# Two-layer graph attention and relation sums: the norm between the layers folded into weights, evictions moved to ScalarE, list writes spread

## The chip, the cores and the metric

The kernel runs on one core of a Trainium2 chip. The metric is the device time of one launch in microseconds; before the change it is 2796.56 us, the median of three runs (2795.64 to 2802.76). The profile is of one further execution. Engines are called PE (matrix multiplies; PEld is its weight load), DVE (the vector engine), ACT (the scalar engine), POOL (GpSimd) and SP (which only issues transfers).

## The reference

There are 1250 nodes with 768 features, 20000 edges sorted by their destination, and 34 edge types. What is computed, cut to what matters:

```python
def gatv2(x, src, dst, Ws, bs, Wd, bd, attn):          # H heads of D features
    fs = (x @ Ws + bs).reshape(-1, H, D)
    fd = (x @ Wd + bd).reshape(-1, H, D)
    logits = einsum('ehd,hd->eh', leaky_relu(fs[src] + fd[dst], 0.2), attn)
    alpha = softmax of logits over the edges of a destination
    return elu(segment_sum(alpha[:, :, None] * fs[src], dst, N))

h   = relu(layernorm(x))
h1  = gatv2(h, ..., W1s, b1s, W1d, b1d, attn1)          # 8 heads of 96
h1  = layernorm(h1 + h) * ln1_w + ln1_b
out = gatv2(h1, ..., Wos, bos, Wod, bod, attno)         # 1 head of 768
x   = x + layernorm(out) * lno_w + lno_b
h   = relu(layernorm(x))
# relation layer: mean over the edges of a type, W_rel[type], sum over types, + h @ W_root + b_rgcn;
# then @ W_gcn, a degree-weighted sum over neighbours, + b_gcn, + x
```

A node without edges has a sum of zero in gatv2, so its elu is zero. Since the attention weights of a node add to one, a constant row added to every fs adds that row to the sum of every node that has edges.

## The kernel before

Nodes are sorted by their number of in-edges and cut into ten tiles of 128. Tile k has as many *slots* as its largest node has edges: 33, 22, 20, 18, 17, 16, 15, 14, 13, 11, in all 179. One slot holds one edge of each of the tile's 128 nodes. Tiles with more than 20 slots are cut into two *chunks* (16 and 17, 11 and 11), so there are twelve chunks.

**Front of the program** (0 to about 150 us): edges are ranked, h and the source rows fs = h @ W1s + b1s are written to memory (f_h0_d and f_fs_d; bias by a matmul of a row of ones with the bias row, line 814).

**First attention** (about 150 to 910 us; `attention(H, ...)`, line 1172, with 8 heads). For a slot, `front` gathers 128 source rows from memory by POOL's indirect transfer (line 1148) into one of 24 ring buffers, and DVE computes max(fs, -fd) (line 1208), the product with attn (1213) and a sum by head (1214). After a chunk's fronts, `softmax` gives the weights, ACT doing the exponent (1232). `back` multiplies the rows by their weights (ACT, eight instructions of 96 columns, line 1266; for the last tile mostly DVE) and PE adds them up in PSUM with two matmuls by the identity (1268). The backs of one chunk alternate with the fronts of the next. `end` then divides by the softmax sum (`share`, line 1276), adds the two chunks of a tile, applies elu and calls `finish1`.

`negated1` (line 1409 on) makes a tile's -fd: POOL gathers h, PE transposes it and multiplies it by W1d, and DVE evicts it from PSUM with the sign and the bias (line 1416). It is called by `begin(j + 2)`, in the middle of chunk j. `finish1` (line 1420 on) adds h, normalizes (statistics on DVE, scaling on ACT, line 1425), multiplies by ln1_w and adds ln1_b (DVE, 1426 and 1427), transposes, multiplies by Wos, evicts with the bias bos (DVE, 1433), makes the row sums of fs times attno, which stand in column 768 (DVE, 1435), scatters fs2 to memory (POOL), multiplies by Wod and evicts with the sign and bod (DVE, 1440). Both denses and negated1's use the one PSUM buffer "mm2". Wos and Wod and five rows, each spread over all 128 partitions, are loaded by `loads1`, called at slot 3 of the first chunk.

**Second attention** (about 910 to 1384 us): the same function with one head. DVE has two instructions a slot (1208, and 1210, which also accumulates), ACT makes a diagonal matrix of the weights (1256) and PE sums with two matmuls (1258). `finish2` (line 1459 on) normalizes, adds x, normalizes again, scatters h2, and multiplies by W_root; it has two elementwise operations (1467, 1470), a gather and two scatters on POOL for each tile.

**List writes.** POOL also writes 179 scatters of 12-byte records into r_pair_d (line 1152), the lists by type which the relation stage reads at its start, after both attentions. `list_edges(row, slots)` adds `slots` to a due counter and issues a write right behind the gather `row` for each whole one. `attention` has two arguments for it: `rate` is added for each slot (not for the first 20 of tile 0), and `rest` once at the last slot. The first attention has 0.9 and 60, the second 0 and 0: 143 writes lie between the gathers of the first attention and 36 behind its last gather.

**Relation stage** (1394 to about 2575 us) and the last sums (to the end) follow; PE sets the pace in the former.

The order of the instructions on an engine is made when the program is built, from the order in which they are written and from where a planner expects an engine to stand idle; so a finish's matmuls have some of the next backs among them. Each engine then runs its own list in order.

Of the kernel before, what the change touches and what calls it, by code (L numbers as in the profile page):

```python
# [10 lines left out]
F32 = mybir.dt.float32  # L11
# [615 lines left out]
def fast_front(ctx, tc, f, x, src, dst, edge_type, W1s, b1s, W1d, b1d, attn1, attno, W_rel):  # L627
# [52 lines left out]
    with ExitStack() as front:  # L680
# [33 lines left out]
        ones_row = early.tile([1, P], F32, name="ones_row")  # L714
# [10 lines left out]
        f.bias_1 = const.tile([P, D], F32, name="bias_1")  # L725
        nc.scalar.dma_start(f.bias_1, bass.AP(tensor=b1d.tensor, offset=b1d.offset, ap=[[0, P], [1, D]]))
# [399 lines left out]
def fast_rest(ctx, tc, f, x, src, dst, edge_type, W1s, b1s, W1d, b1d, attn1, ln1_w, ln1_b,  # L1126
# [45 lines left out]
    def attention(H, table, negated, attn_e, first, loads, finish, rate, rest):  # L1172
# [98 lines left out]
        def share(o, ps, by):  # L1271

            if H == 1:
# [8 lines left out]
        def end(t):  # L1282
# [4 lines left out]
            share(o, c.ps, c.den)  # L1287
# [35 lines left out]
        for j, now in enumerate(chunks):  # L1323
            after = chunks[j + 1] if j + 1 < len(chunks) else None
            for i in range(max(now.n, after.n if after else 0)):
                if i < now.n and after:
                    back(now, i)
                if after and i < after.n:
                    front(after, i)
                if i == now.n // 2:  # L1330
                    begin(j + 2)
            if after:
# [4 lines left out]
            if now.first + now.n == now.t.S:  # L1337
# [7 lines left out]
                            f.degf[:, :, None].to_broadcast([P, NT, S0]), op=ALU.is_ge)  # L1345

# [50 lines left out]
    with ExitStack() as one:  # L1397
        bias_1 = f.bias_1
        late = {}

        def loads1():
            ap1 = late["pool"] = one.enter_context(tc.tile_pool(name="r_att1", bufs=1, side="right"))
            late["wos"], late["wod"] = load_w(ap1, Wos, "wos", "wos"), load_w(ap1, Wod, "wod", "wod")
            for name, a in (("lnw", ln1_w), ("lnb", ln1_b), ("bias_s", bos), ("bias_d", bod), ("attn_o", attno)):
                late[name] = load_row(ap1, a, name)
# [3 lines left out]
        def negated1(k, nfd):  # L1409
# [5 lines left out]
            ps = dense(nc, ps_t, f, hT, f.w1d, 0, P, tag="mm2")  # L1415
            nc.vector.scalar_tensor_tensor(
                nfd.rearrange("p (a h) d -> p a h d", a=2), ps[:, :, :HW].rearrange("p a (h d) -> p a h d", d=D // H),
                -1.0, bias_1.rearrange("p (a h d) -> p a h d", a=2, d=D // H), op0=ALU.mult, op1=ALU.subtract)

        def finish1(k, o):  # L1420
            lnw, lnb, wos, wod = late["lnw"], late["lnb"], late["wos"], late["wod"]
            bias_s, bias_d, attn_o = late["bias_s"], late["bias_d"], late["attn_o"]
# [3 lines left out]
            nc.vector.tensor_mul(o, o, lnw)  # L1426
            nc.vector.tensor_add(o, o, lnb)
            hT = pool.tile([P, KC, P], F32, name="hT1", tag="hT1", bufs=1)
            to_columns(nc, ps_t, f, hT, 0, o, P)
            ps = dense(nc, ps_t, f, hT, wos, 0, P, tag="mm2")  # L1430
            ap1 = late["pool"]
# [296 lines left out]
```

## Time and profile before

| what | value |
|---|---|
| median of three runs | 2796.56 us |
| profiled execution, its own time | 2795.48 us |
| its span | 2793.7 us |
| mean granted clock of PE | 0.925 |
| busy share of PE, DVE, ACT, POOL | 84%, 56%, 30%, 55% |
| first gather of the first, of the second attention | 152.9, 908.8 us |
| last gather of the first, of the second attention | 813.4, 1307.5 us |
| first gather of the relation stage | 1394.6 us |

A row of the groups names line, engine and operation, out<-in with the shapes, the count, then the busy time and the mean in ns of one, then the idle time of the engine just before them and what ended most of it. "issue" is idle time for which the trace shows no wait, "remote" a wait whose releaser it doesn't show. Consecutive DVE instructions overlap by some 0.08 us in these records. Matmuls of fp32 are two records each.

### The profile page before, as it was taken

The numbers are of one execution on the slowest core, as the hardware profiler recorded it, in microseconds if no ns is written. First come the engines' busy times: TensorE is split into PE (matmuls) and PEld (weight loads), VectorE is DVE, ScalarE is ACT, GpSimd is POOL, SyncE is SP. The second block draws the span as 40 slices with busy tenths as digits, with TensorE's granted clock in tenths as the row PEclk, the third lists the DMA queues.
The fourth block names the chain that finished last, engine by engine and source line by source line (L and its number), as shares of the span: only waits on it lengthen the run. The fifth ranks groups of instructions, "written<-read, shape, count | busy, mean of one in ns | idle before, by whom it ended". The sixth has DMA issues, their size and how long they took to land. (4 is left out here: it accounts for less than half of the span.)

```text
span 2793.7 us, 23960 instructions
## 1 busy us (share of the span) xinstructions
PE 2345.4 (84%) x7635; PEld 1354.2 (48%) x7635; DVE 1556.5 (56%) x2363; ACT 851.2 (30%) x2295; POOL 1546.9 (55%) x1131
## 2 busy tenths in 40 slices
PE   5953693788988377898789999999999999999667
PEld 3521252444444244454456666666666666665234
DVE  6589969898985899999453222222222222200263
ACT  3003774776772122333311211221221122121000
POOL 1343877777774766776275444444444544431574
PEclk9976896999999789999889999999999999999888
DMA  6144443454531766765387777777777777765785
GB/s 214 45 159 164 131 129 94 120 142 129 143 102 35 267 208 193 220 208 182 123 264 191 190 191 190 186 195 198 197 188 185 194 192 182 182 158 147 235 275 182
DMA packets 137988, 483.91 MB, mean 173 GB/s; under 512 B 26474, under 2 KB 28803, under 8 KB 137854
## 3 DMA queue, kind: packets, MB, share of 16 engines
q0 software_dynamic: 85152, 341.52, 47.1%
q1 hardware_dynamic: 48043, 134.21, 13.6%
q10 hardware_dynamic: 4658, 6.57, 0.7%
q8 instruction: 63, 1.03, 0.1%
q14 instruction: 72, 0.58, 0.1%
HBM read 392.99 MB, written 89.33 MB: 173 GB/s over the span
## 5 line engine op out<-in xcount | busy, mean ns | idle before, releaser
L1116 PE MATMUL ps<-wrel,mT 128*128 128x384 f32 x3336 | 1099.6, 486 | 1.3 <-DMA wrel<-in_L_gnn_W_rel_dram 1.3
L1116 PEld LDWEIGHTS ps<-wrel,mT 128*128 128x128 f32 x3336 | 623.4, 190 | 407.5 <-issue 1.6
L1148 POOL DMA_INDIRECT g<-r_h_d,lists x241 | 340.8, 1414 | 527.6 <-DVE g L1580 282.8
L1268 PE MATMUL ag<-fs,identf 128*128 128x384 f32 x716 | 291.1, 541 | 178.0 <-ACT fs L1266 167.8
L1580 DVE TENSOR_TENSOR g<-g,g 128x768 f32<-128x768 f32 x68 | 64.6, 950 | 620.4 <-DMA g<-r_h_d,lists 304.0
L1208 DVE TENSOR_TENSOR z<-fs,nfd 128x776 f32<-128x776 f32 (+1 forms) x358 | 347.4, 988 | 45.3 <-DMA fs<-f_fs_d,rec 24.9
L1266 ACT ACTIVATE fs<-fs,lg 128x96 f32<-128x96 f32 x1376 | 371.1, 362 | 4.6 <-issue 4.1
L1258 PE MATMUL ag<-fs,dg 128*128 128x384 f32 x716 | 252.4, 514 | 80.6 <-ACT dg L1256 80.0
L1148 POOL DMA_INDIRECT fs<-f_fs_d,rec x179 | 245.0, 1369 | 104.6 <-issue 48.1
L1152 POOL DMA_INDIRECT r_pair_d<-rec,place x179 | 245.8, 1373 | 95.0 <-issue 47.9
L1268 PEld LDWEIGHTS ag<-fs,identf 128*128 128x128 f32 x716 | 136.4, 205 | 321.1 <-ACT fs L1266 244.4
L1603 POOL DMA_INDIRECT r_h_d<-y,lists x139 | 221.8, 1596 | 109.3 <-ACT y L1602 52.9
L1148 POOL DMA_INDIRECT fs<-r_fs_d,rec x179 | 234.9, 1312 | 83.2 <-issue 33.1
L1258 PEld LDWEIGHTS ag<-fs,dg 128*128 128x128 f32 x716 | 142.1, 201 | 187.6 <-ACT dg L1256 85.7
L1602 ACT ACTIVATE y<-ps,lists 128x768 f32<-128x768 f32 x71 | 64.1, 902 | 479.8 <-PE ps L1116 473.0
L1602 ACT ACTIVATE y<-ps,rcnt 128x768 f32<-128x768 f32 x68 | 61.4, 902 | 456.3 <-PE ps L1116 456.3
L1659 DVE TENSOR_TENSOR acc<-acc,nb 128x768 f32<-128x768 f32 x86 | 82.4, 958 | 198.1 <-DMA nb<-r_h_d,srcz 194.2
L1210 DVE SCALAR_TENSOR_TENSOR z<-z,attn_o 128x769 f32<-128x769 f32 x179 | 178.4, 1015 | 0.0
L1213 DVE TENSOR_TENSOR z<-z,attn 128x776 f32<-128x776 f32 x179 | 168.8, 958 | 0.1
L1214 DVE TENSOR_REDUCE lg<-z 128x8 f32<-128x776 f32 x179 | 168.4, 953 | 0.1
L1513 DVE SCALAR_TENSOR_TENSOR arow<-node,from_f,arow 128x1250 f16<-128x1250 f16 x93 | 140.3, 1508 | 1.0
L1104 PEld LDWEIGHTS pt<-identf,g 128*128 128x128 f32 x834 | 100.5, 142 | 55.2 <-issue 24.1
(284 smaller groups left out, 2301.8 us busy)
## 6 DMA issues: line engine op xcount, KB each, us to landing
wrel<-in_L_gnn_W_rel_dram SPq DMA_DIRECT2D x37, 2304.0 KB
g<-r_h_d,lists POOLq DMA_INDIRECT x241
r_nfd_d<-fd SPq DMA_DIRECT2D x10, 384.0 KB
nfd<-r_nfd_d SPq DMA_DIRECT2D x10, 384.0 KB
r_x_d<-xb SPq DMA_DIRECT2D x10, 384.0 KB
x1r<-r_x_d SPq DMA_DIRECT2D x10, 384.0 KB
f_fs_d<-o_s SPq DMA_DIRECT2D x9, 388.0 KB
x<-in_x_dram SPq DMA_DIRECT2D x9, 384.0 KB
```

The lines of the kernel that those rows point to most:

```text
L1116: last = nc.tensor.matmul(ps[:n, half, :f.HW], hT[:, k, j * P:j * P + n], w[:, k, cols], start=(k == 0), stop=(k == f.KC - 1 and not bias))
L1148: return nc.gpsimd.indirect_dma_start(out=to, out_offset=None, in_=table, in_offset=bass.IndirectOffsetOnAxis(ap=idx, axis=0))
L1152: s = nc.gpsimd.indirect_dma_start(out=table, out_offset=bass.IndirectOffsetOnAxis(ap=idx, axis=0), in_=rows, in_offset=None, **kw)
L1208: nc.vector.tensor_tensor(z, fs, t.nfd, op=ALU.max)
L1210: nc.vector.scalar_tensor_tensor(z[:, 0, :], z[:, 0, :], 1.0, attn_e[:, 0, :], op0=ALU.mult, op1=ALU.mult, accum_out=t.lg[:, s, :])
L1213: nc.vector.tensor_mul(z, z, attn_e)
L1214: nc.vector.tensor_reduce(t.lg[:, s, :], z, axis=AX.X, op=ALU.add)
L1258: nc.tensor.matmul(c.ps[:, half, :HW], dg, fs[:, 0, half * HW:(half + 1) * HW], start=begin, stop=end)
L1266: nc.scalar.activation(fs[:, h, :HD], fs[:, h, :HD], AF.Copy, scale=t.lg[:, s, h:h + 1])
L1268: nc.tensor.matmul(c.ps[:, half, :HW].rearrange("p (h d) -> p h d", d=HD), f.identf, fs[:, half * H // 2:(half + 1) * H // 2, :HD], start= ...
L1513: nc.vector.scalar_tensor_tensor(a, node16, from_f[:, k, s:s + 1], a, op0=ALU.is_equal, op1=ALU.add)
L1603: s = nc.gpsimd.indirect_dma_start(out=h1_d[:, :], out_offset=bass.IndirectOffsetOnAxis(ap=j.node, axis=0), in_=y, in_offset=None, compute ...
```

## The change

It has six parts.

1. `finish1` no longer multiplies by ln1_w and adds ln1_b. `fold(0)` and `fold(1)`, called at slots 5 and 9 of the first chunk's backs (so while the second chunk's fronts run), scale the rows of Wos and Wod by ln1_w in place (ACT, six instructions of 768 columns each). ln1_b @ Wos + bos and ln1_b @ Wod + (ln1_b @ Wos + bos) + bod are made by one-row matmuls and copied out by ACT. ln1_w and ln1_b are loaded as columns, bos and bod as single rows.
2. The source bias ln1_b @ Wos + bos is left out of fs2. It is spread over 128 partitions once (two matmuls, one copy: `bias_s`), and added in `share` to the second attention's sums; to -fd it is added through `late["bias_d"]`. For nodes without edges `finish2` multiplies the norm's scale and shift by `f.has`.
3. Column 768 of fs2, the sum with attno, comes out of the dense: column 768 of Wos is filled once in `fold(0)` (DVE, six instructions), and the second half of the dense has 385 columns.
4. ACT evicts fs2 (two halves), fd2 and nfd in place of DVE; the biases of fd2 and nfd come in by two matmuls with a row of ones.
5. `begin(j + 2)` is called at slot 1 of a chunk, not in its middle.
6. `rate` and `rest` are 0.75 and 0 in the first attention, 0.5 and 60 in the second: 119 writes lie between the gathers of the first, none behind its last gather, and 60 in the second, one for every two slots from slot 20 on.

```diff
@@ fast_front
-        ones_row = early.tile([1, P], F32, name="ones_row")
+        ones_row = f.ones_row = const.tile([1, P], F32, name="ones_row")
...
-        f.bias_1 = const.tile([P, D], F32, name="bias_1")
-        nc.scalar.dma_start(f.bias_1, bass.AP(tensor=b1d.tensor, offset=b1d.offset, ap=[[0, P], [1, D]]))
+        f.bias_1 = const.tile([1, D], F32, name="bias_1")
+        nc.scalar.dma_start(f.bias_1, bass.AP(tensor=b1d.tensor, offset=b1d.offset, ap=[[0, 1], [1, D]]))
+        f.bias_s = const.tile([P, D], F32, name="bias_s")
@@ attention
-        def share(o, ps, by):
-
-            if H == 1:
+        def share(o, ps, by, bias=None):
+
+            if bias is not None:
+                nc.vector.scalar_tensor_tensor(halves(o, P, f), ps[:, :, :HW], by, halves(bias, P, f),
+                                               op0=ALU.mult, op1=ALU.add)
+            elif H == 1:
...
-                if i == now.n // 2:
+                if i == 1:
                     begin(j + 2)
+                if j == 0 and i in (5, 9):
+                    made(i // 9)
@@ loads1, fold
-            late["wos"], late["wod"] = load_w(ap1, Wos, "wos", "wos"), load_w(ap1, Wod, "wod", "wod")
-            for name, a in (("lnw", ln1_w), ("lnb", ln1_b), ("bias_s", bos), ("bias_d", bod), ("attn_o", attno)):
-                late[name] = load_row(ap1, a, name)
+            wos = late["wos"] = ap1.tile([P, KC, W2], F32, name="wos")
+            nc.sync.dma_start(wos[:, :, :D], Wos.rearrange("(k p) n -> p k n", p=P))
+            wod = late["wod"] = load_w(ap1, Wod, "wod", "wod")
...
+            for i, a in enumerate((ln1_w, ln1_b)):
+                nc.scalar.dma_start(cols[:, i, :], bass.AP(tensor=a.tensor, offset=a.offset, ap=[[1, P], [P, KC]]))
...
+        def fold(i):
...
+            ps = ps_t.tile([P, 2, 512], F32, name="b_ps", tag="mm2")
+            for half in range(2):
+                at = slice(half * HW, (half + 1) * HW)
+                for k in range(KC):
+                    nc.tensor.matmul(ps[:1, half, :HW], cols[:, 1, k:k + 1], w[:, k, at], start=(k == 0), stop=False)
+                if i:
+                    nc.tensor.matmul(ps[:1, half, :HW], f.ones_row[:, :1], sums[:, 0, at], start=False, stop=False)
+                nc.tensor.matmul(ps[:1, half, :HW], f.ones_row[:, :1], rows[:, i, at], start=False, stop=True)
+            nc.scalar.copy(sums[:, i, :].rearrange("p (a b) -> p a b", a=2), ps[:1, :, :HW])
+            for k in range(KC):
+                nc.scalar.activation(w[:, k, :D], w[:, k, :D], AF.Copy, scale=cols[:, 0, k:k + 1])
+            if i:
+                return
...
+            nc.scalar.copy(halves(f.bias_s, P, f), ps[:, :, :HW])
+            for k in range(KC):
+                wt = work.tile([P, D], F32, name="wt2", tag="att_e")
+                nc.vector.scalar_tensor_tensor(wt, wos[:, k, :D], SLOPE / (1.0 - SLOPE), f.attn_o[:, 0, :D],
+                                               op0=ALU.mult, op1=ALU.mult, accum_out=wos[:, k, D:])
@@ negated1
-            ps = dense(nc, ps_t, f, hT, f.w1d, 0, P, tag="mm2")
-            nc.vector.scalar_tensor_tensor(
+            ps, _ = dense(nc, ps_t, f, hT, f.w1d, 0, P, tag="mm2", bias=(f.ones_row, f.bias_1))
+            nc.scalar.activation(
...
@@ finish1
-            nc.vector.tensor_mul(o, o, lnw)
-            nc.vector.tensor_add(o, o, lnb)
...
-            nc.vector.tensor_add(halves(fs, P, f), ps[:, :, :HW], halves(bias_s, P, f))
-            wt = work.tile([P, D], F32, name="wt2", tag="att_e")
-            nc.vector.scalar_tensor_tensor(wt, fs[:, :D], SLOPE / (1.0 - SLOPE), attn_o, op0=ALU.mult, op1=ALU.mult,
-                                           accum_out=fs[:, D:])
+            for half in range(2):
+                at = slice(half * HW, HW if half == 0 else W2)
+                for c in range(KC):
+                    nc.tensor.matmul(ps[:, half, :at.stop - at.start], hT[:, c], wos[:, c, at], start=(c == 0), stop=(c == KC - 1))
+                nc.scalar.copy(fs[:, at], ps[:, half, :at.stop - at.start])
...
-            ps = dense(nc, ps_t, f, hT, wod, 0, P, tag="mm2")
+            ps, _ = dense(nc, ps_t, f, hT, wod, 0, P, tag="mm2", bias=(f.ones_row, late["bias_d"]))
-            nc.vector.scalar_tensor_tensor(halves(fd, P, f), ps[:, :, :HW], -1.0, halves(bias_d, P, f),
-                                           op0=ALU.mult, op1=ALU.subtract)
+            nc.scalar.activation(halves(fd, P, f), ps[:, :, :HW], AF.Copy, scale=-1.0)
...
-        attention(H, f.fs_d, negated1, f.attn_1, prepare_lists, loads1, finish1, 0.9, 60)
+        attention(H, f.fs_d, negated1, f.attn_1, prepare_lists, loads1, fold, finish1, 0.75, 0)
@@ finish2
+            for a in (sc, sh):
+                nc.vector.tensor_mul(a, a, f.has[:, k:k + 1])
...
-        attention(1, fs2_d, negated2, f.attn_o, lambda: None, loads2, finish2, 0, 0)
+        attention(1, fs2_d, negated2, f.attn_o, lambda: None, loads2, lambda i: None, finish2, 0.5, 60,
+                  f.bias_s)
```

## The prediction

> **What bounds the kernel now.** I read the page's forty slices first, to find stages, then the table by stage, then the groups of instructions, then single queues in order of time.
>
> The slices of the page (one digit is the busy tenths of a slice of 70 us):
>
> ```profile
> PE   5953693788988377898789999999999999999667
> DVE  6589969898985899999453222222222222200263
> POOL 1343877777774766776275444444444544431574
> ```
>
> DVE stands mostly at 8 and 9 in slices 3 to 19 (a 6 and a 5 stand between), and PE at 9 from slice 22 on. So DVE sets the pace of both attentions (152 to 1384 us) and PE that of the relation stage. The edits lie in the attentions, and the table by stage shows their two steady parts (columns: busy us of PE, PEld, DVE, ACT, POOL; then clock, DMA share, GB/s):
>
> ```profile
> 943.00:1223.00 280.00, 219.66 (x624) 122.97 (x625) 269.37 (x516) 82.04 (x176) 195.59 (x143) 0.88 0.67 205
> 400.00:813.00 413.00, 325.73 (x979) 180.57 (x977) 376.10 (x511) 263.27 (x900) 318.90 (x225) 0.90 0.46 127
> ```
>
> In the first attention (400 to 813) DVE is busy 91%, PE 79%, POOL 77% (and more, as each issue also has a 0.30 us gap before it). In the second (943 to 1223, slots 22 to 141 of its 179) DVE is busy 96%, POOL 70%. The groups give the prices:
>
> ```profile
> L1208 DVE TENSOR_TENSOR z<-fs,nfd 128x776 f32<-128x776 f32 (+1 forms) x358 | 347.4, 988 | 45.3 <-DMA fs<-f_fs_d,rec 24.9 <-DMA fs<-r_fs_d,rec 19.1 <-DVE z L1210 0.4
> L1152 POOL DMA_INDIRECT r_pair_d<-rec,place x179 | 245.8, 1373 | 95.0 <-issue 47.9 <-DMA r_pair_d<-fill 40.7 <-DVE lg L1214 1.5
> ...
> L1148 POOL DMA_INDIRECT fs<-r_fs_d,rec x179 | 234.9, 1312 | 83.2 <-issue 33.1 <-PE ag L1258 23.6 <-DVE mv L1089 9.2
> ...
> L1120 PE MATMUL ps<-bias_r,ones_r 1*128 1x384 f32 x40 | 18.1, 533 | 0.0
> ...
> L1416 DVE SCALAR_TENSOR_TENSOR nfd<-ps,bias 128x768 f32<-128x768 f32 x10 | 9.5, 953 | 26.6 <-remote 18.0 <-PE ps L1116 5.9 <-issue 2.7
> ...
> L1435 DVE SCALAR_TENSOR_TENSOR wt<-fs,attn_o 128x768 f32<-128x768 f32 x10 | 9.5, 952 | 0.1
> ```
>
> A list write (r_pair_d) costs POOL 1.37 + 0.30 us, a gather of the second attention 1.31 + 0.30. How close POOL is to DVE there shows in POOL's own order of time, beside DVE's:
>
> ```profile
> 957.19 1.45 POOL L1148 DMA_INDIRECT fs<-r_fs_d,rec  x1 [0.30 <-DVE z L1210]
> 958.94 1.46 POOL L1148 DMA_INDIRECT fs<-r_fs_d,rec  x1 [0.30 <-PE ag L1258]
> 960.70 1.43 POOL L1148 DMA_INDIRECT fs<-r_fs_d,rec  x1 [0.30 <-DVE z L1210]
> ```
> ```profile
> 959.49 0.95 DVE L1210 SCALAR_TENSOR_TENSOR z<-z,attn_o 128x769 f32<-128x769 f32 x1
> 960.37 0.08 DVE L1210 DVE_READ_ACCUMULATOR z<-z,attn_o 128x1 f32 x1
> ```
>
> Gathers start every 1.75 us, which is two DVE instructions (0.875 us from start to start): POOL finishes one issue per DVE slot and no more. Matching gather k with DVE's k-th z in order of time, z follows its gather by 6.7, 7.6, 6.8, 4.6, 6.9 us at slots 25, 30, 35, 40, 45 and by 4 to 10 us for most of slots 70 to 118; the shortest, about 4 us, is what a gather takes to land. So POOL leads by two or three slots. It has almost no stock.
>
> **First attention, DVE's part.** Per tile finish1 loses the two norm row operations (L1426, L1427), the eviction L1433, the product L1435 and the eviction L1440, and negated1 loses L1416: six of 0.95 us, 0.875 from start to start, plus one accumulator read: 5.3 us. Tiles end (start of att_o, L1276) at 452.8, 522.8, 588.1, 651.1, 706.6, 758.0, 812.6, 856.4, that is every 70.0, 65.3, 63.0, 55.5, 51.4, 54.6, 43.7 us; DVE alone would gain 7 x 5.3 = 37 us. But others come next. PE gets four bias matmuls a tile (two per dense with bias; L1120 gives 18.1 us for ten denses, so 1.8 each): +3.6 us, and it is already busy 50.2 of 51.4 us and 52.9 of 54.6 in the intervals from 706.6 and 758.0; it can follow DVE for the large tiles (57.4 of 70) and hardly for the last. POOL, which had no wait over 0.35 us from 522.8 to 588.1, gets 7% fewer issues (0.75 writes a slot for 0.9). I take 5, 4.3, 4, 4.5, 1.5, 3, 2.7 = **-25 us** (ends -37: PE hides its part; -10: PE keeps its cadence from the fourth interval on). ACT takes over two half evictions, fd and nfd, 0.48 x 2 + 0.9 x 2 = 2.8 us a tile; it is busy 263 of 413 us, so this lies beside DVE. What they queue behind is ACT's scaling of the next slots (16 to 36 of 0.27 us between them in the built order), which itself needs nothing late. The move of nfd to the chunk's head puts its gather before more of POOL's slot gathers, its transposes and dense on PE right behind finish1's two, and takes away the waits of DVE for nfd late in the stage (2.7, 2.3 and 3.6 us at 701, 752 and 804, counted above).
>
> **The fold.** Beside PE: 14 + 16 + 2 matmuls of 384 columns, 0.87 us each at the low clock there (a dense of 12 takes 10.4 us at 174). The first 14 need Wos, issued at 234.5; DMA is saturated until 254 before, and 2 MB of row broadcasts go away, so Wos is there near 243 and the first 14 matmuls end near 255. ACT has three of the six Wos scalings (about 1 us each, as L1425) ahead of its exponent of chunk 0, which ran at 253.8: chunk 0 is scaled from about 257 for 254.2. ACT's other 9 scalings and three copies, 11.5 us, fall into its idle 288 to 300.7. DVE gets six products (0.95) and loses one nfd eviction just before chunk 1's softmax: +4.8 us on the path, at 300. From there to 400 ACT, then PE (finish1's matmuls, then nfd of tile 2), set the pace: no lnw, lnb before the transposes (-1.75), 1.8 us of bias twice. DVE waits for that nfd from 383.1 to 399.4, 8 us longer than PE's matmuls last (to 391.2), and no row says for what; the same wait may or may not return. Sum **+4 us** (-4 to +12). If Wos lands only at 254, as in the old queue, +11 of that end is used.
>
> **The tail of the first attention.** Before, DVE's eviction of tile 8 (878.6) stands in its queue ahead of tile 9's elu and norm, so tile 9's transposes start at 892 and its scatter at 904.9. With ACT evicting, tile 9's norm is done meanwhile; PE goes from tile 8's Wod (887, with bias) straight to tile 9's transposes and Wos, near 897, half a copy of 0.5, scatter near 898: **-7 us** (-3 to -9). The 36 list writes flushed at 815 to 873 cost nothing before: after them POOL waits for DVE:
>
> ```profile
> POOL r_fs_d L1152 <- DVE wt L1435: 29.0, 2, 23.1
> ```
>
> **The list writes.** 0.75 of 159 slots gives 119 writes in the first attention (143 + 36 before); 60 move into the second, one every two slots of 22 to 141, each between gathers on POOL's queue. There POOL is busy 195.6 us, its some 130 issues have 0.30 us each before them (40), so 44 of 280 us are waits: ring (PE ag) 14 beyond those 0.30, mv and den 13, xt 11.6, root 8. Sixty writes: at 1.32 (0.30 and the median 1.02 of the first attention) 79 us; at 1.75, one DVE slot, 105. The Trainium skill (SBUF — State Buffer, § SBUF: two separate sides) says that the port pair shared by DVE and GpSimd is locked for a whole instruction, also by a DVE instruction with two SBUF inputs against a GpSimd one that reads SBUF, and the loser blocks fully. It speaks against this place: the second attention's slot is two such instructions, the first's has a one-input reduction (L1214) as its third. The 1.75 us steps above agree with it. Rule: 236 + 105 + 20 (waits left) = 361, +81. Row: 236 + 79 = 315, less 14 because gathers quicken while DVE idles = 301, +21. As DVE starves it frees the pair, so I take 1.5 a write: 236 + 90 + 10 - 10 = 326, **+46**; I keep +15 to +80. What waits for POOL is DVE's z of every slot, and xt and the h scatter of finish2. The 38 slots after have no writes, but DVE has their full work still, so nothing is won back beyond the lag of 10 us at slot 141 falling to 4 (some 6, inside the range).
>
> **Edits with one answer.** The bias on the sums replaces one share (L1274, 1.009) by one of 0.95; two [128, 1] products a tile for empty nodes, 0.16 us each (as L1094 at 0.19), are 3 us, hidden while DVE waits for POOL; if it doesn't, +3. ones_row and bias rows: nothing on the path. The relation stage and the end are untouched.
>
> **Sum.** Profiled execution 2795.5 us (span 2793.7, 1.8 around it; the median of the runs is 2796.6, 0.04% off): 2795.5 - 25 + 4 - 7 + 46 = **2813.5**.
>
> **Rivals.** (a) POOL absorbs the writes: issues shorten to 1.25 us (as at 909 to 913, with DVE idle) and fill the 44 us of waits. Then the second attention grows by 5 and 2795.5 - 28 + 5 = 2772. It decides (faster at all) where the second attention grows by less than 28 us, 0.47 us a write net of the waits filled. For it: 44 us of waits; against: a lead of two slots. (b) PE (or ACT behind its evictions) takes the first attention's gain as nfd's dense follows finish1's: PE is at 97% in two intervals. 2795.5 + 4 - 7 + 56 = 2848. (c) The change does little: first attention -35, second +35, 2795. (d) The main case.
>
> **How the numbers follow.** 0.3% (8.4 us) is about what a measurement of this kernel can tell. Main case 0.58 (own range 2795 to 2838, of which 0.04 falls within 0.3%), (a) 0.21, (b) 0.14, (c) 0.07. Slower: 0.54 + 0.14 = 0.68; within: 0.04 + 0.07 = 0.11; faster 0.21. The range takes in (a)'s centre and (b)'s: 2772 to 2854.
>
> **What would show it.** DVE idle before z of the second attention waiting for fs from r_fs_d, 40 us or more (19.1 now); list writes there at 1.4 us or above; DVE's end of the second attention about 45 us longer after its first gather; tile intervals of the first shorter by 3 to 5 us, the last ones bounded by PE; its last scatter near 880. Wrong if POOL's issues fall to 1.25 throughout, or if ACT's evictions hold up scaling.

## The result and the profile after

The changed kernel takes 2889.75 us (median of 4 runs, 2884.03 to 2907.03), the kernel before beside it 2799.37: a ratio of 1.0342 (95% interval 1.0306 to 1.0378), 3.4% slower. The direction was right, the 2813.5 us and the range up to 2854 were not. The profiled execution took 2893.91 us with a span of 2892.1, 98.4 longer than the span before. (In the rows of the changed kernel line numbers are higher by one or more: 1209 is 1208 of the kernel before, 1269 is 1268.)

Chips differ: the kernel before had medians of 2799.4, 2784.6, 2795.0, 2788.3 and 2776.3 us in the five sets of runs. So totals are compared as ratios to the kernel before on the same chip, and 0.01 of a ratio is 28 us. Times of stages come from single profiled executions, and the kernel before was profiled in the first set alone, so some us of a stage can be the chip's or the execution's: in the four profiles of one set the first z stands at 181.9 to 198.9 us. Where that matters, stages are counted from the first z.

The slices, page of the changed kernel (now 72 us each):

```profile
PE   5944794788899456778869999999999999999666
DVE  5589958877765787879834222222222222210263
POOL 1233745556660787788636455444445444432474
```

In slices 8 to 11, the middle of the first attention, DVE has fallen to 7 and 8 where it stood at 8 and 9, and no other engine has risen to 9 in its place: PE has 7 and 8, POOL 5 and 6 (PE stands at 9 only behind them, in slices 12 and 13). A loop of waits holds this stage now, not one engine. The table by stage has its tiles 3 to 9 (from the second att_o to the ninth) and slots 20 to 140 of the second attention; columns as before.

```profile
465.00:889.00 424.00, 356.24 (x1062) 193.01 (x1062) 323.38 (x454) 298.55 (x992) 238.84 (x190) 0.93 0.41 115
990.00:1325.00 335.00, 232.44 (x655) 129.32 (x653) 268.74 (x526) 82.41 (x176) 265.09 (x201) 0.84 0.58 167
```

The kernel before, over the same tiles and slots:

```profile
453.00:856.00 403.00, 344.21 (x1025) 190.28 (x1026) 366.04 (x512) 290.85 (x991) 307.78 (x229) 0.92 0.44 122
956.00:1236.00 280.00, 226.54 (x654) 126.60 (x653) 269.37 (x514) 82.33 (x175) 198.45 (x145) 0.90 0.68 204
```

In the first row DVE lost 42.7 us of work and POOL 69, PE gained 12, and the stretch is 21 us *longer*, though PE's granted clock is no lower (0.93 for 0.92). In the second DVE's work is the same to 0.6 us, POOL has 56 instructions and 67 us more, and the stretch is 55 us longer.

| place | before | after | difference | predicted |
|---|---|---|---|---|
| second att_o (fold, chunk heads) | 452.8 | 465.4 | +12.6 | +4 |
| from there to the tenth att_o | 413.0 | 442.2 | +29.2 | -25 |
| tenth att_o to the first z of the second attention | 48.6 | 40.0 | -8.6 | -7 |
| first to last z there | 416.4 | 472.6 | +56.2 | +46 |
| last z to last att_o, and all that follows | | | +9.0 | 0 |

The differences add up to 98.4. (A tile's end begins with its att_o. The z that marks the second attention here is the product with attn_o, line 1210.) Of the table's first row 3.2 us lie ahead of the first z, at 191.7 before and 194.9 after; from there the second att_o comes 9.4 us later. In the last row, 7.8 us lie between the last z and the last att_o (25.9 us before, 33.7 after). The groups of the page show both halves:

```profile
L1209 DVE TENSOR_TENSOR z<-fs,nfd 128x776 f32<-128x776 f32 (+1 forms) x358 | 343.4, 972 | 184.4 <-DMA fs<-r_fs_d,rec 84.9
L1149 POOL DMA_INDIRECT fs<-f_fs_d,rec x179 | 221.9, 1240 | 201.4 <-PE ag L1269 152.6
L1153 POOL DMA_INDIRECT r_pair_d<-rec,place x179 | 245.4, 1371 | 94.0 <-issue 44.9
L1149 POOL DMA_INDIRECT fs<-r_fs_d,rec x179 | 236.9, 1324 | 59.1 <-issue 41.7
```

DVE's idle time ahead of z rose from 45.3 to 184.4 us: 84.9 for rows of the second attention (POOL late with them), 67.0 for rows of the first, and 27.9 for nfd, which ScalarE now writes (21.1 of them once, ahead of the z at 412.9). In the first attention POOL's gathers themselves wait: 152.6 us for PE's sums (`ag`), as a ring buffer may be refilled only when PE has summed the row in it. Waits over tiles 3 to 9 (in total, times, longest), in the kernel before:

```profile
DVE z L1208 <- DMA fs<-f_fs_d,rec: 19.0, 14, 4.4
POOL fs L1148 <- PE ag L1268: 15.8, 18, 4.9
```

and in the changed kernel:

```profile
POOL fs L1149 <- PE ag L1269: 88.2, 31, 10.1
DVE z L1209 <- DMA fs<-f_fs_d,rec: 67.0, 17, 11.6
DVE att_o L1280 <- PE ag L1269: 21.8, 2, 19.5
DVE z L1209 <- ACT nfd L1459: 6.8, 2, 6.6
```

In the stretch from 30 to 53 us behind a tile's end stand two stalls of DVE for three of the tiles, of 6 to 12 us, ten or eleven us apart, and one of 7.5 for a fourth. One of these places in order of time, PE's list behind the second att_o (465.4); columns: start, duration, engine, line, operation, and in brackets the idle time before it and its releaser:

```profile
482.21 4.14 PE L1475 MATMUL ps<-wos,hT 128*128 128x384 f32 x12 [0.28 <-ACT hT L1107]
486.19 0.82 PE L1105 MATMUL pt<-identf,h 128*128 128x128 f32 x6
486.84 0.81 PE L1269 MATMUL ag<-fs,identf 128*128 128x384 f32 x2
487.49 4.04 PE L1475 MATMUL ps<-wos,hT 128*128 128x385 f32 x12
491.37 0.81 PE L1269 MATMUL ag<-fs,identf 128*128 128x384 f32 x2
492.11 4.14 PE L1117 MATMUL ps<-wod,hT 128*128 128x384 f32 x12
496.17 0.91 PE L1121 MATMUL ps<-b_sums,ones_row 1*128 1x384 f32 x2
497.01 4.14 PE L1117 MATMUL ps<-wod,hT 128*128 128x384 f32 x12
501.08 0.91 PE L1121 MATMUL ps<-b_sums,ones_row 1*128 1x384 f32 x2
501.92 1.56 PE L1269 MATMUL ag<-fs,identf 128*128 128x384 f32 x4
503.31 4.03 PE L1117 MATMUL ps<-f_w1d,hT 128*128 128x384 f32 x12
507.27 0.91 PE L1121 MATMUL ps<-bias,ones_row 1*128 1x384 f32 x2
508.11 4.14 PE L1117 MATMUL ps<-f_w1d,hT 128*128 128x384 f32 x12
```

and in it the gathers of POOL and the z of DVE that waited longest (other rows left out):

```profile
487.93 0.98 POOL L1149 DMA_INDIRECT fs<-f_fs_d,rec  x1 [4.56 <-PE ag L1269]
503.10 0.99 POOL L1149 DMA_INDIRECT fs<-f_fs_d,rec  x1 [9.42 <-PE ag L1269]
514.20 0.98 POOL L1149 DMA_INDIRECT fs<-f_fs_d,rec  x1 [8.82 <-PE ag L1269]
```
```profile
507.20 0.97 DVE L1209 TENSOR_TENSOR z<-fs,nfd 128x776 f32<-128x776 f32 x1 [11.63 <-DMA fs<-f_fs_d,rec]
518.14 0.97 DVE L1209 TENSOR_TENSOR z<-fs,nfd 128x776 f32<-128x776 f32 x1 [7.98 <-DMA fs<-f_fs_d,rec]
```

For 30 us PE works through three denses and their biases, with sums (`ag`) worth two slots between them: a slot has two matmuls, each of them two records. The gather at 503.10 had waited 9.42 us for a row that the sum at 501.92 freed; it landed 4 us later, and let DVE, idle for 11.63 us, do one more slot of 3.0 us. ScalarE isn't what is late here: by 513 it has scaled the rows of some fifteen slots of this chunk and PE has summed five, and from then on PE does 53 records of sums in 17.4 us without a gap. So DVE goes at the pace at which PE gets to the sums. Why it has no stock there: a chunk has 11 to 20 slots and the ring 24 rows. When a softmax is done the chunk's own rows are all still held, and only the remainder is ahead of DVE.

### The profile page after: what moved, and what is told of

The parts are those of the page before. It is cut to its first block, busy times and chain, and to the rows that moved or that the text cites. A ratio compares the mean times of both kernels' runs of the same rounds, so it can differ in the third digit from the quotient of the medians.

```text
span 2892.1 us, 24238 instructions
## 1 busy us (share of the span) xinstructions
PE 2409.2 (83%) x7779; PEld 1372.8 (47%) x7779; DVE 1506.5 (52%) x2326; ACT 885.9 (31%) x2350; POOL 1511.7 (52%) x1131
## 5 line engine op out<-in xcount | busy, mean ns | idle before, releaser
L1209 DVE TENSOR_TENSOR z<-fs,nfd 128x776 f32<-128x776 f32 (+1 forms) x358 | 343.4, 972 | 184.4 <-DMA fs<-r_fs_d,rec 84.9
L1269 PE MATMUL ag<-fs,identf 128*128 128x384 f32 x716 | 281.6, 536 | 110.6 <-ACT fs L1267 78.8
L1149 POOL DMA_INDIRECT fs<-f_fs_d,rec x179 | 221.9, 1240 | 201.4 <-PE ag L1269 152.6
L1107 ACT COPY mT<-pt 128x384 f32<-128x384 f32 x278 | 119.0, 485 | 26.9 <-PE pt L1105 26.9
```

The source lines that it names most:

```text
L1149: return nc.gpsimd.indirect_dma_start(out=to, out_offset=None, in_=table, in_offset=bass.IndirectOffsetOnAxis(ap=idx, axis=0))
L1209: nc.vector.tensor_tensor(z, fs, t.nfd, op=ALU.max)
L1269: nc.tensor.matmul(c.ps[:, half, :HW].rearrange("p (h d) -> p h d", d=HD), f.identf, fs[:, half * H // 2:(half + 1) * H // 2, :HD], start= ...
```

## The experiments

The largest question was which of the six parts did it, and whether through VectorE, as the prediction had it, or through the ring. (VectorE is the DVE of the rows, ScalarE their ACT.) Parts 1 to 3 and the biases on PE stay together in what is called the fold; nfd begun at slot 1 is called the head. Every edit also makes the order of the instructions anew, so a difference between two runs holds that as well.

**One line each way: where nfd is begun.** The edit on the changed kernel, and its mirror image on the kernel before:

```diff
-                if i == 1:
+                if i == now.n // 2:
                     begin(j + 2)
```

> The changed kernel with one line undone: nfd of the chunk after next is again begun in the middle of a chunk instead of at slot 1. Theory 1 (a burst on PE: finish1's two denses and nfd's dense now stand back to back, few sums of slots get between them, the ring of 24 rows is not freed, gathers and then DVE starve): the two stalls of DVE of about 7 us behind each tile's end go, the last att_o of the first attention starts near 850 instead of 907.6 us, and the kernel takes about 2835 us (2820 to 2850). Theory 2 (ScalarE's evictions, which wait for PE, hold up the scaling of slots behind them in ScalarE's order): the stalls stay, only spread out, the last att_o stays above 895 us and the kernel above 2875. Theory 3 (the fold in the second chunk makes the start later and the rest follows): same as theory 2 here, with the 11 us of the first tile's end kept.

e1 measured 1.0244 (1.0203 to 1.0286) against 1.0342: 27 us come back, the tenth att_o starts at 878.5 instead of 907.6, and POOL's waits for sums over tiles 3 to 9 fall from 88.2 to 37.7 us. This is about half of what theory 1 asked for. The waits of z for rows fell from 67 to 35 us, and 23.2 us of waits for nfd, which ScalarE now writes, stand beside them. So the burst is real, but it is not all.

> The kernel before with that one line changed alone: nfd begun at slot 1 of a chunk; VectorE still evicts, list writes and norm as before. Theory 1: the burst on PE is there too, waits of z for rows from f_fs_d in the first attention grow from 25 to 70 us or more, and the kernel takes 2840 to 2860 us. Theory 2: VectorE's evictions do not queue ahead of the scaling, so no more than 10 us are lost: 2790 to 2807. In between (2810 to 2835): both have a part.

e2 measured 1.0075 (1.0051 to 1.0098), +21 us: both theories' middle. From the first z to the tenth att_o it took 691.5 us, 17 more than in the profile before. But the waits of z for rows of f_fs_d rose only from 24.9 to 33.5 us, where theory 1 had 70 or more.

**The list writes.** `0.75, 0` and `0.5, 60` in the two calls against `0.9, 60` and `0, 0`.

> The changed kernel with the list writes spread as before (0.9 a slot and 60 at the end in the first attention, none in the second). If the second attention's 56 us (from its first z to its last, 416.4 before and 472.6 after) come from the 60 writes on POOL's queue: it goes back to 412 to 420 us, the first attention stays as in the changed kernel within 8 us, and the kernel takes about 2832 us (2820 to 2845). If part of them comes from the sums' bias and the two [128, 1] products or from scattered rows that arrive late: over 430 us, and the kernel above 2850.

In this run, e3, the second attention did go back, to 415.5 us; the writes are all of its 56. But the kernel only went to 1.0293 (1.0252 to 1.0335), since the first attention became longer by what had not been expected: its tenth att_o starts at 939.8, 32 us later than in the changed kernel, and 753.0 us behind the first z for 712.8.

> The kernel before with the new spread of list writes alone (0.75 and 0, then 0.5 up to 60). Writes as the cause: the second attention takes 465 to 478 us from its first z to its last, the first attention gains 0 to 8 us as its POOL has fewer issues, total about 2850 us (2840 to 2862). If POOL could absorb the writes in the kernel before, whose gathers wait less for late rows: under 2825.

e4 measured 1.0159 (1.0119 to 1.0199), +44 us, and 472.9 us from the first z to the last. The groups of that kernel:

```profile
L1208 DVE TENSOR_TENSOR z<-fs,nfd 128x776 f32<-128x776 f32 (+1 forms) x358 | 342.4, 968 | 97.4 <-DMA fs<-r_fs_d,rec 73.0
L1152 POOL DMA_INDIRECT r_pair_d<-rec,place x179 | 254.3, 1420 | 94.5 <-issue 41.5
```

DVE's wait for rows of the second attention is there (73.0, before 19.1) with nothing else of the change. What the second attention lost, the first gave back in part: its tenth att_o came at 853.3 for 865.8, which is 654.3 us behind the first z for 674.2. Counted so, fewer writes help the first attention by 20 us in the kernel before, and by 40 in the changed one. That POOL has more to catch up there, after each stall, would explain the second figure; it wasn't tried.

**Who evicts.** ScalarE's three evictions back on VectorE, with nfd in the middle (e5) and at the head (e6), new list writes:

```diff
-                nc.scalar.copy(fs[:, at], ps[:, half, :at.stop - at.start])
+                nc.vector.tensor_copy(fs[:, at], ps[:, half, :at.stop - at.start])
...
-            nc.scalar.activation(halves(fd, P, f), ps[:, :, :HW], AF.Copy, scale=-1.0)
+            nc.vector.tensor_scalar(halves(fd, P, f), ps[:, :, :HW], -1.0, None, op0=ALU.mult)
```

> The run with nfd begun in the middle of a chunk, and besides VectorE, not ScalarE, evicts fs, fd and nfd (plain copies and a multiplication by -1; fold, bias on PE and the new list writes stay). Between the tile ends 1 and 10 (second to last att_o) the run with ScalarE took 416 us and the kernel before with the same list writes 404. Theory A (ScalarE's scaling frees the ring's rows just behind a softmax, and evictions that sit in its order there delay it; VectorE would have waited for rows anyway): 395 to 405 us, the waits of z for rows from f_fs_d fall from 35 to 20 us or less, and the kernel comes 12 to 25 us below the run with ScalarE. Theory B (what is lost sits in the fold and the first two tiles; ScalarE's evictions are free): within 6 us of the run with ScalarE, and still 410 us or more between those ends.

e5 measured 1.0248 (1.0229 to 1.0266), the same as with ScalarE (1.0244). Theory B holds for the total, A falls (417.8 us between the ends, 24.7 of waits for rows): moving the evictions is worth nothing in either direction when nfd is in the middle.

> The changed kernel (nfd at slot 1, new list writes) with VectorE as the evicting engine. Theory A with the burst: nfd at the head costs the kernel before only some 8 us of its first attention but the changed kernel 29, because there ScalarE evicts all three denses at the head; with VectorE the first attention's last att_o comes near 875 instead of 907.6 and the kernel 25 to 40 us below the changed kernel (about 2850 to 2865 on the chip of the prediction). Theory B: the head alone is what costs: the last att_o stays above 895.

e6 measured 1.0276 (1.0258 to 1.0293), 18 us below the changed kernel, the tenth att_o at 890.0: between the theories. The head costs 8 us more than the middle when VectorE evicts (1.0276 against 1.0248, intervals that overlap) and 27 when ScalarE does. In the profiles the difference lies between the second and the tenth att_o (+7.7 us and +25.9); in the second attention the head takes 8 to 12 us off in both and adds 10 or 11 behind its last z. ScalarE's own waits for PE's denses over tiles 3 to 9 don't explain it: 33 us with the head and 33 with the middle. Why the two prices differ stays open.

**Fewer writes without the second attention.** In the kernel before, 0.8 for 0.9 a slot:

> The kernel before with 0.8 list writes a slot instead of 0.9 in the first attention, and all the others (52 instead of 36) at its end. 0.75 a slot took the first attention from 674 to 654 us (first z to last att_o); in proportion 0.8 should take 10 to 14 us. If the longer flush at the end still lies in the 23 us for which POOL waited for the scatter: the kernel is 6 to 14 us faster than before. If the flush reaches past the last scatters (16 more writes of 1.6 us are 26): no gain, 0 to 8 us slower.

e7 measured 1.0039 (1.0025 to 1.0054), slower. The first attention gained its 15 us (659.1 from the first z to the tenth att_o, 674.2 before), but the second's first z came 72.3 us behind that att_o instead of 48.6. VectorE's waits there:

```profile
DVE fs L1433 <- DMA r_fs_d<-fs,f_perm: 30.8, 1, 30.8
DVE fs L1433 <- PE ps L1116: 8.7, 1, 8.7
```

The writes flushed at the end ran to 886 us (873.6 before), and the scatter of an earlier tile's rows is behind them on POOL's queue. There is one buffer for these rows, so VectorE's next eviction waited 30.8 us for that scatter, and PE's next dense behind it. So a flush 12 us longer cost 24: the 23 us for which POOL waited for VectorE were no cover, since VectorE in turn waits for what is behind the flush on POOL's queue. The flush of the kernel before just had room: without any (e4) the same step takes 48.7 us.

**The fold.** With VectorE evicting, nfd in the middle and no writes in the second attention, at 0.8 (e8) and 0.9 (e10) writes a slot:

> Fold and bias by PE kept, VectorE evicts, nfd in the middle of a chunk, list writes 0.8 a slot and the rest at the first attention's end, none in the second. The fold then takes 2.6 us of VectorE's work (lnw, lnb, the product for the logit's column) off each tile of the first attention and adds the bias to the sums of the second, against some 10 to 15 us that the first tile ends later. Theory A: within 8 us of the kernel before with 0.8 alone. Theory B: 12 to 25 us slower than that.

e8 measured 1.0145 (1.0118 to 1.0173), 30 us slower than the kernel before with 0.8 alone. Neither theory had that much.

> The same with the fold at slots 5 and 9, as in the changed kernel: fold and bias on PE alone, against the kernel before. From the pairs run so far (fold against none at 0.75 and at 0.8 writes a slot): 20 to 30 us slower than before, of which 15 in the first tile and 8 to 14 in the others, less 5 to 8 at the end of the first attention. If the fold costs only together with fewer list writes: within 10 us of before.

e10 measured 1.0085 (1.0057 to 1.0113), +24 us, as expected. So the fold, though it takes work off VectorE, costs 24 to 30 us. Two runs took it apart. First, the four bias matmuls a tile left out, so fd and nfd lack their biases:

```diff
-            ps, _ = dense(nc, ps_t, f, hT, wod, 0, P, tag="mm2", bias=(f.ones_row, late["bias_d"]))
+            ps = dense(nc, ps_t, f, hT, wod, 0, P, tag="mm2")
```

> The same, and the four bias matmuls a tile on PE left out (fd and nfd then lack their biases, so part of the computation is missing). Theory P (behind a tile's end PE's chain of denses is what VectorE waits for): tiles 2 to 9 become shorter by most of 3.6 us each, 15 to 28 us in all. Theory R (rows freed late by ScalarE): up to 10 us, as PE's sums come only a little sooner. If VectorE is the limit: under 4 us.

e11 measured 1.0006 (0.9993 to 1.0018), 22 us faster than with them. The stages of tiles 3 to 9 with the bias matmuls, and then without:

```profile
475.00:885.00 410.00, 365.53 (x1080) 197.58 (x1081) 349.90 (x491) 292.17 (x997) 276.45 (x228) 0.94 0.42 119
```
```profile
470.00:854.00 384.00, 337.06 (x1025) 189.73 (x1026) 349.21 (x491) 290.29 (x991) 285.35 (x229) 0.95 0.45 128
```

VectorE's work is the same, PE's is 28.5 us less, and the stretch is 26 us shorter: 3.7 us a tile for four matmuls of about 0.9. Theory P holds: these matmuls were on the path in full, though PE is busy only 89% of that stretch. VectorE's waits moved with it, for rows (25.9 to 15.3 us) and for PE's denses (27 to 16). Without these matmuls the fold costs nothing that this run can tell from the kernel before.

> The fold with VectorE evicting, nfd in the middle of a chunk and the list writes of the kernel before, with one more edit: the fold's two parts are issued at slots 12 and 16 of the first chunk loop instead of 5 and 9. With the fold at 5 and 9 the first tile ended 15 to 16 us later, counted from the first z, since ScalarE has Wos and Wod to scale (12 us) before it can scale the slots whose rows the ring waits for. Theory R (ScalarE's time counts because rows are freed late): at 12 and 16 it falls into ScalarE's idle time ahead of the second softmax, the first tile ends 150 to 156 us after the first z instead of 166, and the kernel is 8 to 14 us faster than with the fold early. Theory D (the six products on VectorE and the later nfd are what costs): no more than 4 us are won.

e9 measured 1.0069 (1.005 to 1.0089) for the fold at slots 12 and 16, against 1.0085 at 5 and 9: less than was expected (4 us for the 8 to 14 of theory R), and the intervals overlap. The profiles of this pair show the first softmax's exponent 59.3 and 66.6 us after the first z, and the second att_o 13 us sooner with the late fold. But even so the first tile ends 165.4 us after the first z (169.5 with the early fold, 152.9 before, 150 to 156 by theory R). So theory R isn't borne out, and what holds the rest of that start isn't settled.

**The ring.** Fewer rows in the kernel before:

```diff
-        ring = 24
+        ring = 20
```

> The kernel before with 20 rows in the ring instead of 24. Theory R: chunks have 11 to 20 slots, so behind a softmax only the rows beyond the chunk's own are ahead of VectorE; four fewer make it wait for rows 5 to 10 us more in each tile with 16 slots or more, 30 to 70 us in the first attention. Theory V, the prediction's (VectorE sets the pace, POOL leads by what a gather takes to land): under 10 us there.

e12 measured 1.0374 (1.0346 to 1.0403): four rows fewer cost 104 us, more than the whole change. VectorE's wait for rows over tiles 3 to 9:

```profile
DVE z L1208 <- DMA fs<-f_fs_d,rec: 52.3, 26, 4.7
```

(19.0 with 24 rows). From the first z to the tenth att_o the kernel takes 718.3 us instead of 674.2, the second attention 460 instead of 416. Theory R holds: the kernel before, too, lived on the ring.

**Turned into a kernel.** The last three runs ask whether this gives time back. e13 keeps the fold and takes the biases off PE: the fold's matmuls have the shift as 128 equal columns, so that the folded biases stand on all partitions, and VectorE subtracts them while it evicts.

```diff
+            for k in range(KC):
+                lb = work.tile([P, P], F32, name="lb", tag="dg", bufs=3)
+                nc.vector.tensor_copy(lb, cols[:, 1, k:k + 1].to_broadcast([P, P]))
+                for half in range(2):
+                    at = slice(half * HW, (half + 1) * HW)
+                    nc.tensor.matmul(ps[:, half, :HW], lb, w[:, k, at], start=(k == 0), stop=(k == KC - 1))
+            b = (f.bias_s, late["bias_d"])[i]
+            nc.vector.tensor_add(halves(b, P, f), ps[:, :, :HW], halves(b, P, f))
...
-            fd = ap1.tile([P, D], F32, name="fd2", tag="fd2", bufs=1)
-            nc.scalar.activation(halves(fd, P, f), ps[:, :, :HW], AF.Copy, scale=-1.0)
-            nc.sync.dma_start(nfd2_d[k * P:(k + 1) * P, :], fd)
+            nc.vector.scalar_tensor_tensor(halves(o, P, f), ps[:, :, :HW], -1.0, halves(late["bias_d"], P, f),
+                                           op0=ALU.mult, op1=ALU.subtract)
+            nc.sync.dma_start(nfd2_d[k * P:(k + 1) * P, :], o)
```

> The fold without bias matmuls on PE: the folded biases stand on all partitions (the fold's own matmuls have the norm's shift as 128 equal columns, VectorE adds) and VectorE subtracts them as it evicts, as in the kernel before; fold at slots 12 and 16, nfd in the middle, list writes as before, fd written into the tile that the norm is done with. Theory P (PE's chain behind a tile's end is what the rows and VectorE wait for): tiles 2 to 9 take some 384 us as in the run with the bias matmuls left out (410 with them), and the kernel comes within 8 us of the one before (2788). If leaving the biases out changed the time otherwise than by PE's 3.6 us a tile: still above 400 us for these tiles.

Tiles 3 to 9 take 383.1 us, as with the biases left out, and the kernel is *faster* than the one before: e13 measured 0.9954 (0.994 to 0.9968), 13 us where no more than 8 either way had been expected. It is a second, complete way to take the bias matmuls off PE, and has the same effect on these tiles.

> The same with 27 rows in the ring instead of 24, in the room that the folded rows have left. Theory R (rows come free late behind a softmax): 4 rows fewer cost the kernel before 3.7%, so 3 more should give back a third to the whole of that rate: 25 to 75 us less than with 24 in both attentions together. Theory V (VectorE's own work is what is left of the time once PE's chain is short): under 8 us.

e14 measured 0.9903 (0.9884 to 0.9922), 1.0% faster than the kernel before and the fastest of all, but only 15 us below e13, between the two theories. VectorE's waits over tiles 3 to 9 say why; first e13 with 24 rows, then e14 with 27:

```profile
DVE z L1209 <- DMA fs<-f_fs_d,rec: 15.3, 14, 4.4
DVE nfd L1454 <- PE ps L1117: 9.3, 3, 6.4
DVE fs L1471 <- PE ps L1470: 4.3, 3, 2.4
```
```profile
DVE fs L1471 <- PE ps L1470: 20.5, 6, 7.1
DVE nfd L1454 <- PE ps L1117: 10.1, 4, 5.3
DVE z L1209 <- DMA fs<-f_fs_d,rec: 4.0, 4, 1.7
```

The waits for rows went, and VectorE waits for PE's dense instead: the tiles take 386.3 us, no less. The gain lies in the second attention (421.0 to 410.2 us) and between the two (46.0 to 38.4).

> The kernel before with 25 rows in the ring (the room comes from writing fd into the tile that the norm is done with), nothing else. Theory R: 8 to 25 us faster than before. Theory V: within 5 us.

e15 measured 0.9947 (0.9928 to 0.9965): one row more makes the kernel before 15 us faster, as theory R has it. Over tiles 3 to 9 VectorE's elapsed time less its gaps is 367.9 us for 367.8 before, and the wait for rows is down from 19.0:

```profile
DVE z L1208 <- DMA fs<-f_fs_d,rec: 7.9, 11, 1.6
```

That fd is written to another tile is part of this run too; its own share wasn't measured.

## Why the prediction was wrong

Undoing the change in one order gives its parts as ratios: list writes +44 us (1.0159), fold and biases on PE +25 (1.0248), ScalarE evicting 0 (1.0244), nfd at the head +27 (1.0342). The parts aren't independent (e3, e6), so another order shares the 96 us out otherwise. Set beside the predicted 2813.5, the profiled execution came 80 us too long; in the rows of the table above, 54 of them lie in the first attention, 10 in the list writes, 9 in the fold and 9 behind the last z, and the tail gave 2 back.

**First attention, -25.** This is the step that failed: +29.2 was measured. VectorE's part of it was right. Over tiles 3 to 9, elapsed time less the gaps of over 0.15 us ahead of VectorE's instructions:

| kernel | elapsed | VectorE idle | the rest |
|---|---|---|---|
| before | 403.6 | 35.8 | 367.8 |
| list writes alone (e4) | 394.2 | 26.2 | 368.0 |
| + fold, biases on PE (e5) | 409.5 | 59.0 | 350.5 |
| + ScalarE evicts (e1) | 403.5 | 71.3 | 332.2 |
| + nfd at the head (after) | 423.8 | 99.7 | 324.1 |

The prediction took 37 us off VectorE, and it lost 43.7, of which some 7 are seven scalings of the last tile's rows that lie behind the ninth att_o in the changed kernel and ahead of it in the others. Its waits grew by 63.9. "DVE sets the pace of both attentions" was read from a busy share of 91% over the stage. That average hides the first 50 us behind a tile's end, where rows come one by one as PE frees them, and it was there that the work was removed (finish1) and there that PE's work was added. The kernel before was held by the ring as well, as one row more (e15, 15 us faster) and four fewer (e12, 104 slower) show. The text put the end of this step at -10, "PE keeps its cadence", and excluded a loss without a reason for it; the 3.6 us of bias matmuls a tile it had counted correctly and then let PE hide at the large tiles (e11: all of it was on the path). The room for it was read from PE's busy times of 57.4, 50.2 and 52.9 us in three intervals, which are 54.7, 47.5 and 50.5 in the profile before; PE had even more idle time than was thought, and it didn't help. That nfd's dense comes "right behind finish1's two" was written down and given no price; the head cost 27 us (e1). Rival (b) named PE, but let it only take the gain; that it could also cost, through the ring, was in no case.

**ScalarE's evictions, beside DVE.** Right as a cost with nfd in the middle (e5, nothing), but not with the head, where VectorE evicting is 18 us faster (e6); and wrong as a gain: the time that VectorE was spared became waiting.

**Fewer writes in the first attention.** They had no value in the sum; e4 shows 20 us for the kernel before, counted from the first z.

**The fold, +4 (-4 to +12).** The second att_o came 12.6 us later, but 9.4 counted from the first z, which is inside. The term for the first exponent was undersized: three scalings ahead of it were counted, 2.6 us by the profile of e10, but not the 1.28 us of a table load between them and the exponent; the profile before has none right ahead of that exponent, but one at 237.6, 16 us ahead of it. The scalings "fall into its idle 288 to 300.7" only in part: e9's later place brought the second softmax 7.6 us nearer. The wait for nfd up to 399.4, of 16.3 us, was left open and came back as the 21.1 us ahead of 412.9.

**The tail, -7.** The size was right: -8.6 from the tenth att_o to the second attention's first z. The mechanism isn't shown. With VectorE evicting and no flush (e5) the gain is as large (40.2 us for 48.7 in e4), so ScalarE isn't needed for it there; with the flush kept it is there with ScalarE and the head (e3, 40.0) and gone with VectorE and the middle (e10, 48.9).

**The list writes, +46 (+15 to +80).** The mechanism was right, the size 10 us short, within its bounds. POOL was the bound: busy 265.1 of 335 us with 201 instructions, and at 0.30 us ahead of each some 60 more. That leaves 10 us of waits, as the sum had it. The 143 issues beside the writes took 186.3 us, for 195.6 of as many in the prediction's stretch, so they did quicken, by 9 us for the 10 that were taken off. What was too small is the write: 1.5 us with the gap ahead of it was taken, and it took 1.36 and 0.30. The low end of that choice, 1.02, was a median of the first attention; the mean there was 1.40 before, as some writes take up to 4.3 us, and a queue's sum goes by means. The exclusive lock of the port that DVE and POOL share (the Trainium skill, SBUF — State Buffer, § SBUF: two separate sides) would have had 361 us in the prediction's own working, 26 more than was measured. No run here tests the port itself: in the changed kernel the median write is 1.50 us in the second attention and 1.04 in the first, but the mean is 1.37 in both.

**Rival (a)**, POOL absorbing the writes, fell with e4. **What would show it** came true for the second attention: waits of 84.9 us for r_fs_d, writes at a median of 1.50 (the mean, 1.37, is just below the 1.4), DVE's end 56 us later behind its start. The intervals of the first attention were to shrink by 3 to 5 us; five grew (70.0 to 76.2, 65.3 to 68.6, 63.0 to 65.5, 55.5 to 63.2, 51.4 to 61.0) and the last two shrank (54.6 to 51.6, 43.7 to 37.6). Its last scatter was to come near 880 and came at 938.8.

**Behind the last z, 0.** It was +9.0, nearly all of it ahead of the last att_o. That comes 33.7 us behind the last z with the fold and the head, 21.5 with the fold alone (e1) and 23.9 with the head alone (e2), so it takes both; the prediction had looked at the head in the first attention only.

## What to carry to other kernels

Where a ring of buffers feeds an engine, the engine's busy share over a stage doesn't say that it sets the pace (91% here): look for the moment at which the ring is emptiest (here behind each softmax) and ask which engine frees the next buffer. Here work removed from the fed engine at that moment turned into waiting, and work added to the freeing engine, even four matmuls of 0.9 us a tile, counted in full. Memory that a rewrite sets free may be worth more as buffers than the instructions that it saves: one row of 3 KB a partition was worth 0.5% here.

## What was not expected of the hardware

ScalarE's scalings of a row, 0.27 us apart in long stretches, go 0.70 us apart in some, with nothing that the profile shows to wait for. From the order of time of e10:

```profile
337.00 0.38 ACT L1267 ACTIVATE fs<-fs,lg 128x96 f32<-128x96 f32 x1 [0.34 <-issue]
337.71 0.38 ACT L1267 ACTIVATE fs<-fs,lg 128x96 f32<-128x96 f32 x1 [0.34 <-issue]
338.42 0.37 ACT L1267 ACTIVATE fs<-fs,lg 128x96 f32<-128x96 f32 x1 [0.33 <-issue]
```

Such gaps sum to 10.8 us between 300 and 420 us there, to 9.8 in the changed kernel, 4.1 in the kernel before, 7.2 in e2, which has no fold, and none in e4. They lie in the first tiles, where the part of the fold's cost lies that no run explained. They can't be all of that: e13 has the fold and none of these gaps, and its first tile still ends 162.2 us after the first z, for 152.9 before. Whether they are a part of it wasn't tried.
